# Fourier-layer passes with fewer TensorE instructions, 1 MB transfers and another order of steps

## The chip, the cores and the metric

The kernel runs on one core of a Trainium2 chip. The time is the device time of one execution in microseconds (us), and the median of several runs is quoted. The core has five engines that work side by side, each through its own instructions in order: TensorE (PE, matrix products; its weight loads are listed as PEld), VectorE (DVE), ScalarE (ACT), GpSimd (POOL) and SyncE (SP). SP computes nothing here: it issues most of the DMA transfers, which 16 DMA engines carry between device memory (DRAM) and the on-chip memory SBUF. TensorE writes its results into PSUM, from where DVE and ACT read them. Semaphores order the engines among each other.

## The reference

64 images of 256 x 256 go through a Fourier neural operator with 32 channels and 4 layers. Its output is joined with 77 text rows per image, and one transformer layer (attention and a routed feed-forward part) follows. The part that the change touches is the operator:

```python
v = h @ p_w + p_b                                  # 3 -> 32 channels
for i in range(L):                                 # L = 4
    x_ft = jnp.fft.rfft2(v)                        # only 24 x 12 frequencies are kept
    out1 = jnp.einsum('bixy,ioxy->boxy', x_ft[:, :, :M1, :M2], W1)
    out2 = jnp.einsum('bixy,ioxy->boxy', x_ft[:, :, -M1:, :M2], W2)
    ...
    x1 = jnp.fft.irfft2(out_ft, s=(Sx, Sy))
    x2 = jnp.einsum('bcxy,cd->bdxy', v, w_w[i]) + w_b[i]
    v = x1 + x2
    v = (v - mean) * rsqrt(var + eps) * bn_g[i] + bn_b[i]   # statistics over the whole batch
    if i < L - 1:
        v = relu(v)
out = jnp.einsum('bcxy,cu->bxyu', v, q_w) + q_b
```

Everything is 32-bit floating point. Because the normalisation needs statistics of the whole batch before any value can be normalised, the layers can't be fused for one image: all 64 images pass through one layer before the next begins.

## The kernel before

The program has four kinds of stages. The first (forward_first) takes the input images to their low frequencies. Between layers stands mix (about 160 us in the trace from the last image of one pass to the first of the next), which multiplies the frequencies with the weights and works out the statistics. Three passes (layer, i = 0, 1, 2) turn the mixed frequencies of layer i back into an image, apply normalisation and relu, and take the result forward to the frequencies that the next layer needs. Last comes the transformer, image by image. The change lies in layer. Pass 0 has an order of steps of its own. Passes 1 and 2, the later passes, share one order, and the pass number is i.

**One image in a later pass.** An image is cut into 8 tiles t. A tile is 128 partitions (four row groups of 32 channels) times 8 rows of 256 columns, 1 MB. In DRAM a partition's 8 rows lie together. These are the steps, by the names that the order uses; a digit behind a step is its tile:

- ld (L655): loads the old v of a tile into a vin buffer (4 buffers), as two DMAs of four rows each.
- am (L646): loads the mixed frequencies of an image (ams, two buffers) and scales them on POOL. sp (L663) expands them along x, two matmuls into one ring buffer, spT (L672) transposes that on DVE into y. There are two halves, sp0 for tiles 0 to 3 and sp1 for tiles 4 to 7.
- pre (L681): the new v before relu: 8 matmuls with a 24-row contraction (L687) plus 16 of 32 x 32 that add W v (L698). It allocates the tile's vo buffer (4 buffers).
- evA, evB (L705): relu from PSUM into vo, half a tile each, on ACT (letter a, L710) or DVE (letter d, L712).
- st (L716): stores vo to DRAM, as two DMAs of four rows.
- turn (L721): a 32 x 32 block transpose of vo on DVE (L724) into t32, for the transform along y.
- prod (L729): the next layer's W times v, 16 matmuls of 32 x 32 (L735). Row group n writes PSUM bank ps[n]. sqA and sqB (L741) then sum the squares of the result on ACT (L746), for the variance.
- y0 to y7 (L750): the transform along y over all tiles, 16 matmuls each (L757), all into two ring buffers. half and zt0, zt1 (L764, L770) take the result out through ACT and DVE.
- x (L783): the transform along x, 12 matmuls of 128 x 128 weights times 96 columns (L791) for three groups of frequencies; xo (L800) copies it out on ACT, xs (L807) stores it.

In the profile a 32-bit matmul appears as two MATMUL instructions, each with its own LDWEIGHTS: the 16 of a prod are 32 rows.

**PSUM ring.** The whole of PSUM is four ring buffers of two banks each. take (L605) gives a step the buffers that were closed longest ago: two for pre, prod and y, one for sp and x. close (L617) stands in the eviction step that frees one. So which eviction a matmul step waits for follows from the order alone.

**Order.** ORDER (L128) is written out by hand: one string for pass 0, one for the later passes. The loop at L834 runs the string once per image b; @1 behind a step means that it is done for image b+1, @-1 for image b-1. Each engine executes its own part of this list in exactly this order, and SP issues the DMAs in it, each when what it waits for is done. Steps of different images are thus interleaved: while image b finishes its tiles and its y, image b+1 is begun.

## Time and profile before

| what | value |
|---|---|
| time, median of 3 runs | 11274.06 us (11268.07 to 11280.38) |
| the profiled execution | 11266.44 us, span 11264.7 us, granted TensorE clock 0.984 |
| busy: PE, DVE, ACT, POOL | 10600.1, 8446.4, 6475.0, 1448.0 us |
| PE instructions in the profile | 182550 |
| DMA | 3457.30 MB, mean 307 GB/s |
| pass 0, per image | about 36 us |
| later passes, per image | about 45 us, 128 images |
| transformer, all images | from about 8600 us on |

The profiled execution is one run with the hardware profiler; all durations of instructions come from it. Busy time is the union of the times in which an engine executed something; matmuls are pipelined, and their ends are modelled. The page's 40 slices are 281.6 us each, and a digit is the busy share of a slice in tenths. A line of the groups or of the timeline names the source line, the engine, the operation, the tile written and those read, and the shapes. What stands behind an arrow at the end is what ended the engine's idle time before it. "Share" in a DMA line is the part of the 16 DMA engines' time that the queue's packets took.

### The profile page before, as it was taken

To read this page: it belongs to the slowest core of one execution; us is meant where nothing else is said; L and a number is where in the kernel's file an instruction comes from. 1 tells how busy PE (TensorE), PEld (TensorE's weight loads), DVE (VectorE), ACT (ScalarE), POOL (GpSimd) and SP (SyncE) were. 2 spreads that over 40 slices of the span, in tenths; PEclk is the share of its full clock that TensorE was granted. 3 is DMA by queue.
4 is the path that set the end of the run, shared out by engine and by line. 5 is a ranking of instruction groups with operands and counts; after the bars stand their busy time and mean duration, and the time that the engine had idled before them with its cause. 6 is when DMAs were issued, how large, how long until landed. Compare 5 with 4: busy or idle time off the path is not lost.

```text
span 11264.7 us, 409247 instructions
## 1 busy us (share of the span) xinstructions
PE 10600.1 (94%) x182550; PEld 5728.7 (51%) x182550; DVE 8446.4 (75%) x10381; ACT 6475.0 (57%) x10673; POOL 1448.0 (13%) x2179
## 2 busy tenths in 40 slices
PE   6999999998999999999799999999996999999999
PEld 3555555554444444444444444444443666666666
DVE  6888888887777777777677777777776666666665
ACT  5777777775656555566556566556664333333333
POOL 1111111110000000000000000000000333333333
PEclk8999999998999999999999999999998999999999
DMA  6776676678999999999899999999998555555553
GB/s 214 248 248 246 246 249 246 246 252 322 381 383 384 378 379 375 376 379 379 316 366 386 379 376 381 382 380 378 375 379 301 224 228 228 225 226 227 225 227 137
DMA packets 971776, 3457.30 MB, mean 307 GB/s; under 512 B 149016, under 2 KB 198552, under 8 KB 903064
## 3 DMA queue, kind: packets, MB, share of 16 engines
q1 hardware_dynamic: 904576, 3366.80, 77.7%
q0 software_dynamic: 58288, 60.60, 2.3%
q8 instruction: 1429, 23.41, 0.8%
q10 hardware_dynamic: 7144, 3.72, 0.1%
q14 instruction: 339, 2.78, 0.1%
HBM read 1733.60 MB, written 1696.92 MB: 305 GB/s over the span
## 4 chain that ended last, share of the span: by engine, by line
PE 61%; DMA 21%; DVE 9%; ACT 4%; issue 3%; SPq 2%; POOL 0%; ACTq 0%; DVEq 0%; POOLq 0%
PE ring L757 15%; DMA v<-vo 11%; PE ring L687 9%; PE ring L735 8%; DMA vin<-v 6%; PE ring L698 5%; PE hp L992 4%; PE ring L667 3%; PE pp L1155 3%; PE pp L1166 3%; PE ring L791 2%; PE pp L1120 2%; DVE vo L712 2%; PE pp L1185 2%; DMA xh<-xo 2%
## 5 line engine op out<-in xcount | busy, mean ns | idle before, releaser
L746 ACT ACTIVATE ring<-ring 128x1024 f32<-128x1024 f32 x3072 | 3115.9, 1014 | 1176.6 <-PE ring L735 1114.9
L724 DVE STREAM_TRANSPOSE t<-vo 128x2048 f32<-128x2048 f32 x1536 | 3465.4, 2286 | 21.1 <-DVE vo L712 0.9
L735 PE MATMUL ring<-vo,w 32*32 32x512 f32 x49152 | 2401.5, 599 | 80.3 <-ACT vo L710 64.2
L712 DVE TENSOR_SCALAR vo<-ring 128x1024 f32<-128x1024 f32 x1280 | 1543.8, 1221 | 1191.4 <-PE ring L698 805.3
L710 ACT ACTIVATE vo<-ring 128x1024 f32<-128x1024 f32 x1792 | 1792.2, 1023 | 1039.9 <-PE ring L698 498.1
L757 PE MATMUL ring<-t,cst 32*32 32x512 f32 x49152 | 2063.5, 599 | 46.4 <-issue 40.2
L757 PEld LDWEIGHTS ring<-t,cst 32*32 32x32 f32 x49152 | 909.6, 103 | 917.1 <-issue 615.9
L735 PEld LDWEIGHTS ring<-vo,w 32*32 32x32 f32 x49152 | 801.3, 103 | 1064.7 <-issue 397.6
L687 PE MATMUL ring<-cst,y 24*128 24x256 f32 x16384 | 1232.6, 403 | 76.8 <-DVE vo L712 59.5
L634 POOL TENSOR_TENSOR ams<-ams,bns 48x512 f32<-48x512 f32 x384 | 401.1, 1045 | 6964.8 <-DMA ams<-mix 6692.2
L698 PE MATMUL ring<-vin,ws 32*32 32x512 f32 x32768 | 1278.0, 603 | 17.9 <-issue 14.0
L687 PEld LDWEIGHTS ring<-cst,y 24*128 24x128 f32 x16384 | 789.8, 185 | 992.8 <-DVE vo L712 389.1
L675 DVE STREAM_TRANSPOSE y<-ring 128x1024 f32<-128x1024 f32 x384 | 762.7, 1986 | 320.0 <-PE ring L667 319.0
L687 PE MATMUL ring<-mv,y 29*128 29x256 f32 x8192 | 705.1, 403 | 36.6 <-ACT ring L746 20.2
L687 PEld LDWEIGHTS ring<-mv,y 29*128 29x128 f32 x8192 | 455.9, 185 | 370.2 <-ACT ring L746 209.8
L791 PEld LDWEIGHTS ring<-cst,zt 128*128 128x128 f32 x4608 | 533.6, 193 | 176.7 <-ACT vo L710 113.8
L767 ACT COPY half<-ring 128x1024 f32<-128x1024 f32 x192 | 194.5, 1013 | 723.9 <-PE ring L757 723.9
L1193 POOL DMA_DIRECT2D out_dram<-o x1024 | 511.2, 508 | 664.8 <-DVE o L1188 622.9
L746 ACT ACTIVATION_READ_ACCUMULATOR ring<-ring 128x1 f32 x3072 | 585.4, 191 | 0.0
L791 PE MATMUL ring<-cst,zt 128*128 128x96 f32 x4608 | 565.6, 280 | 6.2 <-DVE zt L775 6.0
L775 DVE STREAM_TRANSPOSE zt<-ring 128x1024 f32<-128x1024 f32 x192 | 377.4, 1965 | 242.8 <-PE ring L757 242.8
L667 PE MATMUL ring<-ams,cst 49*128 49x512 f32 (+1 forms) x1536 | 450.4, 641 | 108.7 <-POOL ams L634 40.1
(374 smaller groups left out, 9759.8 us busy)
## 6 DMA issues: line engine op xcount, KB each, us to landing
v<-vo SPq DMA_DIRECT2D x3072, 512.0 KB, 7.9
vin<-v SPq DMA_DIRECT2D x2048, 512.0 KB, 9.0
ch<-v SPq DMA_DIRECT2D x512, 1024.0 KB, 13.9
mix<-ob SPq DMA_DIRECT2D x48, 1024.0 KB, 5.3
ams<-mix SPq DMA_DIRECT2D x384, 96.0 KB, 8.0
xin<-in_x_dram SPq DMA_DIRECT2D x16, 1024.0 KB, 8.2
mv<-in_x_dram POOLq DMA_DIRECT2D x256, 64.0 KB, 7.2
out_dram<-o POOLq DMA_DIRECT2D x1024, 16.0 KB, 3.1
```

Source lines behind the costliest of these rows:

```text
L667: nc.tensor.matmul(ps[:, n, :], lhsT=EX[hv, 128 * h:128 * h + 128], rhs=ams[b % 2][hv], start=True, stop=True, skip_group_check=True,)
L675: nc.vector.transpose(y_[b, h].rearrange("p q c -> p c q"), ring[key][0][1].rearrange("p n (c k) -> p (n c) k", k=32),)
L687: nc.tensor.matmul(ps[n][:, 256 * r:256 * r + 256], lhsT=y_[b, t // 4][32 * n:32 * n + K, q:q + 4, :].rearrange("p q c -> p (q c)"), rhs=m ...
L698: nc.tensor.matmul(ps[n][32 * j:32 * j + 32], lhsT=ws[32 * n:32 * n + 32], rhs=v[32 * n:32 * n + 32, 2 * j:2 * j + 2, :], start=False, sto ...
L710: nc.scalar.activation(to, ring[key][h][1], AF.Relu)
L712: nc.vector.tensor_scalar(to, ring[key][h][1], 0.0, None, ALU.max)
L724: nc.vector.transpose(t32[b, t // 2][:, :, 8 * (t % 2):8 * (t % 2) + 8, :].rearrange("p y s c -> p s y c"), vo[b, t].rearrange("p s (y l) ...
L735: nc.tensor.matmul(ps[n][32 * j:32 * j + 32], lhsT=w4[i + 1][32 * n:32 * n + 32], rhs=vo[b, t][32 * n:32 * n + 32, 2 * j:2 * j + 2, :], st ...
L746: nc.scalar.activation(ps, ps, AF.Square, accum_out=acc[:, at:at + 1])
L757: nc.tensor.matmul(ps[n][32 * j:32 * j + 32], lhsT=FYT[32 * n:32 * n + 32, k, :], rhs=t32[b, j][32 * n:32 * n + 32, k].rearrange("p s c -> ...
L791: nc.tensor.matmul(ps[:, 0, 96 * g:96 * g + 96], lhsT=zt_[:, h, k0:k0 + 4, :].rearrange("p k c -> p (k c)"), rhs=FX[:, h, 48 * r:48 * r + ...
L1193: nc.gpsimd.dma_start(out[b, 64 * n + 16 * g:64 * n + 16 * g + 16].rearrange("(p t) d -> p t d", t=2), o[32 * g + 8 * n:32 * g + 8 * n + 8 ...
```

## The change

Later passes get these edits:

- **Transfers.** ld is one DMA of 1 MB instead of two of 512 KB, in SP's queue as before; so is st when i is 1 or 2.
- **Wide products.** A prod with the letter w, which the new order uses for tiles 1 and 7, is 8 matmuls of 64 x 64 instead of 16 of 32 x 32. Its weights w64 are built once in a pass: 64 x 64 blocks with W twice on the diagonal and zeros beside it. Both row halves write into the same bank, ps[j], on different partitions.
- **x transform.** Where the order has xt, x takes the table FX as weights (64 columns) and zt as the moving operand (384 columns): 4 matmuls. The result is turned the other way round; xe copies it to SBUF on DVE, and xt turns it back with 3 matmuls against ID2, two stacked identities, which also add the two halves. That makes 7 matmuls instead of 12.
- **Order.** The later passes' string is replaced. Sixteen evictions have the same split as before, 9 on ACT and 7 on DVE. Per image and pass the order now begins with the evictions of pre2, runs pre4, pre5, pre3, pre7, pre0 and pre1 before y0, puts pre6 between y1 and y2, prod1 between y4 and y5, and prod7 behind y7, and ends with pre2 of the image after next. Loads, stores, am and xs move with it.

In pass 0 the order, x and the stores stay as they are.

```diff
 ), (
-    "pre5 sqB7@-1 zt1@-1 sqA7@-1 pre6 evA5.a ld2@1 st4 evB5.d st5 turn4 evA6.a prod5 x@-1 "
-    "evB6.a sqB5 prod6 sqA5 xo@-1 turn5 pre2@1 sqA6 turn6 sqB6 prod4 evA2.a@1 evB2.d@1 "
-    "sqB4 ld0@1 ld7 sqA4 pre0@1 evB0.d@1 ld3@1 prod2@1 st6 evA0.a@1 turn2@1 sqB2@1 sqA2@1 "
-    "pre3@1 ld1@1 evA3.a@1 st2@1 evB3.d@1 pre7 evB7.d prod3@1 ld5@1 evA7.a sqA3@1 turn7 "
-    "pre1@1 st0@1 am@2 sqB3@1 prod0@1 evA1.a@1 evB1.d@1 sqA0@1 st7 sp1@1 st1@1 ld4@1 y0 "
-    "spT1@1 y1 ld6@1 turn0@1 turn3@1 xs@-2 y2 sqB0@1 prod1@1 y3 sqB1@1 sp0@2 y4 sqA1@1 "
-    "spT0@2 y5 y6 st3@1 turn1@1 y7 half.a pre4@1 zt0 prod7 evB4.d@1 evA4.a@1 "
+    "evA2.a@1 evB2.a@1 ld5 ld7 pre4 ld0@1 turn6 prod6 evA4.a x@-1 evB4.d xe.d@-1 turn4 "
+    "sqA6 sqB6 prod4 xt@-1 st2@1 turn2@1 sqA4 pre5 sqB4 xo@-1 am@2 evA5.d evB5.a pre3@1 "
+    "prod2@1 evA3.d@1 turn5 evB3.a@1 st4 sqA2@1 pre7 sqB2@1 evA7.a prod5 evB7.d xs@-1 "
+    "sqB5 pre0@1 ld1@1 st5 sqA5 st3@1 prod3@1 turn7 evB0.a@1 sp1@1 sqA3@1 evA0.d@1 pre1@1 "
+    "sqB3@1 spT1@1 evA1.a@1 prod0@1 ld6@1 sqA0@1 evB1.d@1 ld2@2 sp0@2 spT0@2 y0 ld4@1 y1 "
+    "st1@1 sqB0@1 turn3@1 turn0@1 pre6@1 y2 evB6.d@1 y3 evA6.a@1 y4 prod1.w@1 sqB1@1 st7 "
+    "sqA1@1 y5 st0@1 y6 st6@1 turn1@1 y7 prod7.w half.a zt0 sqA7 sqB7 ld3@2 pre2@2 zt1 "
 )]
...
+    ID2 = const.tile([128, 2 * KX], F32, name="id2")
+    nc.vector.tensor_add(ID2, ID[:, 0:2 * KX], ID[:, 64:64 + 2 * KX])
...
+            w64 = cp.tile([128, 2, C], F32, name="w64")
+            nc.vector.memset(w64, 0.0)
+            for n in range(4):
+                nc.vector.tensor_copy(w64[32 * n:32 * n + 32, n % 2, :], w4[i + 1][32 * n:32 * n + 32])
+            w64 = w64.rearrange("p n o -> p (n o)")
...
+            turned = "xt" in ORDER[min(i, 1)]
...
                 vin[b, t] = ip.tile([128, 8, S], F32, name="vin")
-                for n in range(2):
-                    rows = slice(4 * n, 4 * n + 4)
-                    nc.sync.dma_start(vin[b, t][:, rows], src[b][:, t, rows])
+                nc.sync.dma_start(vin[b, t], src[b][:, t])
...
             def st_(b, t, e):
+                if i:
+                    nc.sync.dma_start(dst[b][:, t], vo[b, t])
+                    return
                 for n in range(2):
...
             def prod(b, t, e):
                 take(("prod", b, t), 2)
                 ps = banks(("prod", b, t))
+                if e == "w":
+                    for j in range(4):
+                        for n in range(2):
+                            m = (n + j) % 2
+                            nc.tensor.matmul(
+                                ps[j][64 * m:64 * m + 64], lhsT=w64[64 * n:64 * n + 64],
+                                rhs=vo[b, t][64 * n:64 * n + 64, 2 * j:2 * j + 2, :], start=True, stop=True,
+                                skip_group_check=True,
+                            )
+                    return
                 for k in range(4):
...
             def x_(b, n, e):
                 zt_ = zts.pop(b)
                 ps = take(("x", b), 1)[0]
+                if turned:
+                    for r in range(2):
+                        for h in range(2):
+                            nc.tensor.matmul(
+                                ps[64 * h:64 * h + 64, 0, 0:384], lhsT=FX[:, h, 48 * r:48 * r + 64],
+                                rhs=zt_[:, h, M * r:M * r + M, :].rearrange("p k c -> p (k c)"),
+                                start=r == 0, stop=r == 1, skip_group_check=True,
+                            )
+                    return
                 for g in range(3):
...
-            xos = {}
+            xos, xes = {}, {}
+
+            def xe(b, n, e):
+                xes[b] = xp.tile([128, 384], F32, name="xe")
+                if e == "a":
+                    nc.scalar.copy(xes[b], ring["x", b][0][1][:, 0, 0:384])
+                else:
+                    nc.vector.tensor_copy(xes[b], ring["x", b][0][1][:, 0, 0:384])
+
+            def xt(b, n, e):
+                xe_ = xes.pop(b)
+                for g in range(3):
+                    nc.tensor.matmul(
+                        ring["x", b][0][1][:, 1, 96 * g:96 * g + 2 * KX],
+                        lhsT=xe_[:, 128 * g:128 * g + 128], rhs=ID2, start=True, stop=True,
+                    )
```

xo then reads the second bank of the ring buffer where the order has xt, and the first as before where it has not.

More of the change, by code (lines that the diff above doesn't have):

```diff
@@ L802, in xo @@
                 nc.scalar.copy(
-                    xos[b], ring["x", b][0][1][:, 0, 0:288].rearrange("p (g k) -> p g k", g=3)[:, :, 0:2 * KX]
+                    xos[b], ring["x", b][0][1][:, int(turned), 0:288].rearrange("p (g k) -> p g k", g=3)[:, :, 0:2 * KX]
                 )
@@ L811, in layer @@
                 am=am, lx=lx, ld=ld, sp=sp, spT=spT, pre=pre, evA=ev(0), evB=ev(1), st=st_, turn=turn,
-                prod=prod, sqA=sq(0), sqB=sq(1), y=y, half=half, zt0=zt(0), zt1=zt(1), x=x_, xo=xo, xs=xs,
+                prod=prod, sqA=sq(0), sqB=sq(1), y=y, half=half, zt0=zt(0), zt1=zt(1), x=x_, xe=xe,
+                xt=xt, xo=xo, xs=xs,
             )
```

## The prediction

> **What bounds the kernel now.** I read the page's slices first. Slices 9 to 19 and 20 to 30 are the two later passes, the only stretch that the new order, the new x and the large transfers touch:
>
> ```profile
> PE   6999999998999999999799999999996999999999
> ...
> DMA  6776676678999999999899999999998555555553
> GB/s 214 248 248 246 246 249 246 246 252 322 381 383 384 378 379 375 376 379 379 316 366 386 379 376 381 382 380 378 375 379 301 224 228 228 225 226 227 225 227 137
> ```
>
> In these passes both TensorE and the DMA engines stand at nine tenths. A window of 2000 us inside one pass, and the DMA view of the same window (packets, MB, share; then transfers, KB, us to landing), say how full. In the first line PE's busy time comes first, then PEld, DVE, ACT, POOL, the granted clock, DMA share and GB/s:
>
> ```profile
> 3400.00:5400.00 2000.00, 1915.79 (x40907) 906.36 (x40912) 1501.38 (x839) 1204.04 (x1897) 92.05 (x88) 1.00 0.98 379
> ```
>
> ```profile
> q1 hardware_dynamic: 215029, 751.33, 97.2%
> ...
> v<-vo SPq DMA_DIRECT2D x706, 512.0 KB, 8.9
> vin<-v SPq DMA_DIRECT2D x704, 512.0 KB, 9.0
> ```
>
> PE is busy 95.8%, DMA 98%. The window has 44.1 images (706 stores, 16 an image), so one image takes 45.35 us. A 512 KB transfer alone would need 1.4 us at 379 GB/s; it lands after 9, so six stand in line: DMA is saturated. Its queue was busy 0.972 x 45.35 = 44.1 us an image, instruction fetches 0.5: a floor of 44.6.
>
> But PE busy counts the tail of every matmul, so I also took the starts of its groups from the timeline:
>
> ```profile
> 4410.14 3.40 PE L757 MATMUL ring<-t,cst 32*32 32x512 f32 x96
> ...
> 4424.00 1.49 PE L735 MATMUL ring<-vo,w 32*32 32x512 f32 x32
> ...
> 4425.49 2.92 PE L791 MATMUL ring<-cst,zt 128*128 128x96 f32 x24
> ...
> 4428.34 1.14 PE L735 MATMUL ring<-vo,w 32*32 32x512 f32 x32
> ...
> 4429.41 1.16 PE L687 MATMUL ring<-cst,y 24*128 24x256 f32 x16
> ...
> 4430.51 1.14 PE L698 MATMUL ring<-vin,ws 32*32 32x512 f32 x32
> ...
> 4431.80 1.02 ACT L710 ACTIVATE vo<-ring 128x1024 f32<-128x1024 f32 x1
> ...
> 4431.86 1.22 DVE L712 TENSOR_SCALAR vo<-ring 128x1024 f32<-128x1024 f32 x1 [1.72 <-PE ring L698]
> ```
>
> Start to start without a wait, a pre is 1.08 (L687) + 0.88 us (L698), a prod 0.88, one y 1.1; a change of array shape adds 0.19 (0.88 becomes 1.07). Evictions start 1.3 us after L698 does; then an ACT pass takes 1.0, a DVE eviction 1.23, turn 2.29, spT and zt 2.0. With four PSUM ring buffers, two for each pre, prod or y, a step waits for the eviction two steps back. From the starts of PE's groups, least (mean) per image: x+prod6 3.92 (3.92), pre2+prod4 3.54 (3.55), pre0+prod2 3.71 (3.90), pre3 2.16 (2.52), pre7+prod3 3.71 (4.12), pre1+prod0 3.45 (3.89), sp1 to y3 6.83 (7.34), sp0 to y7 5.54 (6.02), pre4+prod7 3.71 (4.39), pre5 2.16 (2.24), pre6+prod5 3.45 (3.51). Sum 42.2 (45.4). So the chain through PE, ACT, DVE and the ring could do 42.2; the DMA floor of 44.6 is what holds an image at 45.35. Where the wait appears, the waits of that window show:
>
> ```profile
> ACT vo L710 <- DMA v<-vo: 98.9, 68, 3.3
> ...
> DVE vo L712 <- DMA v<-vo: 93.2, 68, 3.3
> ```
>
> Evictions wait for a store that still reads their vo buffer.
>
> **The change, part by part (us per image of a later pass).**
>
> *1 MB transfers.* 32 issues become 16, the bytes stay; a partition's run goes from 4 KB to 8 KB. In the packet records of the window a 4 KB packet takes 159 ns at best, 168.6 on average. 8 KB packets are in the trace too, the ch loads of the last stage: 309 at best, 319.3 on average. The DMA view there (9500 to 10500 us) agrees:
>
> ```profile
> q1 hardware_dynamic: 32386, 215.24, 53.2%
> ...
> ch<-v SPq DMA_DIRECT2D x200, 1024.0 KB, 13.9
> ```
>
> 215.24 MB in 0.532 of 1000 us is 405 GB/s of busy time, against 751.33 / (0.972 x 2000) = 386 now. Per engine, 255 packets x 168.6 = 43.0 become 127.5 x 319.3 = 40.7, or 41.8 if the excess over the best case (9.6 ns) grows with the bytes (328). With 1.4 for the rest: a floor of 42.1 to 43.3, I take 42.7, a gain of 1.3 to 2.5 in the floor. The nearest row is all reads, hence the far end: no gain. There a rule of the Trainium skill speaks against the change ("DMA: Bandwidth & Descriptors", Specifications): HBM gives one core about 358 GB/s. Were that the limit, packet size would buy nothing and the floor stay at 44.6. The trace moves 379 through both passes, above the figure, and its busy time falls per packet; I go by the rows. A store now waits for both halves of a tile; they are evicted within 0.3 us of each other on two engines, and no store's landing is due sooner than four tiles later.
>
> *x turned.* Removed: 24 instructions x 112 ns = 2.69. Added: 8 of 128x64 by 384 columns. The first stage's L239 has that shape with 512 columns: two column halves run side by side, 429 ns a round. So 4 rounds x 322 = 1.29; then xt, 6 x 112 = 0.67 (128 weight columns as in L791); two more shape changes, 0.4. PE gains 0.3. DVE's xe (128x384, about 0.5 between the 128x144 copy's 0.28 and the eviction's 1.23) holds turn4 behind it, 1.5 us idle before x has landed; turn4 is needed only by y, 20 us on. prod4 stands between x and xt and hides xe.
>
> *Two wide products.* 32 instructions become 16, each of 64x64 with half its weights zero. No row shows 64x64. By L735 the array holds sixteen 32x32 at once (853 ns for 32), so four 64x64 at 429 a round make 16/4 x 429 = 1.72: that end is +0.86 each, plus two shape changes for prod1 and one for prod7. The other end: the two row halves write the same bank (ps[j]), where the old code gives each row group its own (ps[n]). The skill's "TensorEngine Tiling (Array Packing)", PSUM Pressure, says that different row tiles cannot access one bank at the same time; then two run at once, 3.43. Its page "PSUM — Partial Sum Buffer" (bank collisions) quotes that each bank of each partition is a memory of its own, and the halves here never share a partition. No row decides; I take 1.72, as column halves sharing a bank at L239 cost nothing, and keep 3.43 for the range.
>
> *The order.* Priced by the same walk, t from pre2's start, each step at the later of PE free and ring released (0.07 after the eviction ends). pre2 0; pre4 2.15; prod6 4.37 (waits for evA2 and evB2, both ACT behind sqA7, sqB7); x 5.6 (evA4); prod4 7.1; xt 8.2; pre5 9.55 (sqA4); pre3 11.7; prod2 13.66; pre7 15.36 (evA3); prod5 17.3; pre0 19.0 (evB7); prod3 20.96; sp1 22.45; pre1 23.5; prod0 25.72 (spT1); sp0 26.97; y0, y1 28.17; pre6 30.4; y2 to y4 32.4; prod1 wide 36.05 (evB6 behind spT0, turn3, turn0 on DVE: 0.4); y5 to y7 38.0, done 41.1; prod7 wide; pre2 again 2.47 later, when zt0 is done. That is 43.6, against 42.2 for the old order: +1.4, nearly all from the wide products. Of prod7's, 0.37 lies under zt0.
>
> SP's queue, same clock: ld7 2.0 (buffer of pre2), ld0 4.2, st2 4.4, am, st4 5.8, xs 10.8, ld1 13.7, st5, st3 and ld6 15.5, ld2 17.3, ld4 21.0, st1, st7 and st0 27.3, st6, ld3, ld5 36. xs now waits for xo with ld1 behind it, but ld1's buffer is free only at 13.7. st7 sits behind st1 for 8 us; its buffer is asked for at 46. At 2.6 us a transfer, each load lands at least 5 us before its pre, each store 1.5 or more before the eviction that reuses its buffer: tightest st5, 20.4 against evA1 at 25.9, and st2 with evA7, 11 against 17.7. So this order does not wait for DMA. am moves ahead, which drops sp0's wait for ams (30 us in the window, 0.7).
>
> *Setup.* w64 is five small DVE instructions a pass, ID2 one in all: 3 us at most, in front of the first pre.
>
> **Sum.** New image: the chain's 43.6, above the DMA floor of 42.7, plus 0.5 because the two lie within a microsecond of each other (the old pair, 2.4 apart, ran 0.8 over the larger): 44.15. That is 1.1 below the 45.25 of the 124 undisturbed periods, 136 us. The profiled execution took 11266.4 us (span 11264.7, 1.7 around it); it becomes 11130, or 11138 by the median of 11274, which lies 7.6 above.
>
> **Rivals.** (a) The wide products' halves exclude each other: at 3.43 each, prod1 costs 1.7 more and prod7 1.4: 47.2 an image, +2.0 x 124 = 248, 11520, slower. It decides from 2.45 us a product on, where (s - 1.72) + (s - 2.09) eats the 1.1. For it: the shared bank and the cited rule; against: separate partitions. (b) DMA stays the bound: 8 KB packets in a mix of reads and writes are no faster per byte, 45.3, 11270, no change. For it: the 8 KB rows are all reads; against: 9 ns less overhead per 4 KB at best case. (c) PE gains more than streaming says: runs of y take 1.1 a step where prod takes 0.88, with pauses of 0.2 after each 32 matmuls; if those are instruction supply, runs of two or three y, broken by long products, drop them: 43, -2.2 x 124, 11000.
>
> **How the numbers follow.** My case 0.54 (own range 11030 to 11220: 43.3 to 44.9 an image), (a) 0.25, (b) 0.11, (c) 0.10. Less than 0.2% (22 us) either way is not told from no change. Faster: 0.52 of my case and (c), 0.62; same: 0.08, most of (b); slower: (a) and what errs in my case or (b), 0.30. The range 11000 to 11420 leaves out the worst of (a) and the best of (c).
>
> **What would show it.** Right: DMA share near 0.95 and about 390 GB/s in the passes, waits of evictions for v<-vo almost gone, wide product groups 1.7 us from start to start plus 0.2, xt 0.7. Wrong: wide products over 2.4 us; DMA share still 0.98 at 380 GB/s; pre5 waiting for sqA4, or prod1 for evB6, much over the 0.5 given them.

## The result, and the profile after

The changed kernel takes 11214.48 us (median of 4 runs, 11213.23 to 11222.15) against 11273.67 for the kernel before, run beside it: 59 us less, ratio 0.9948 (95% interval 0.9933 to 0.9963). It is faster, by less than half of the 136 us forecast. Run again beside the kernel before, twice, it gave 11206.35 against 11274.82, ratio 0.9938 (0.9923 to 0.9953), and 11214.23 against 11271.06, ratio 0.9945 (0.9928 to 0.9961).

The page's slices of the changed kernel (span 11212.1 us, granted clock 0.984; a slice is 280.3 us). The later passes are again slices 9 to 19 and 20 to 30:

```profile
PE   6999999997999999999799999999997999999999
...
DMA  6767766678999999999899999999997555555553
GB/s 211 248 244 250 248 245 248 247 248 321 377 385 385 379 383 386 389 380 385 316 358 389 380 385 378 390 386 381 386 386 293 227 226 226 226 226 226 226 227 136
```

TensorE and the DMA engines still both stand at nine tenths. The same 2000 us window as before (PE, PEld, DVE, ACT, POOL busy, granted clock, DMA share, GB/s), and then its DMA view:

```profile
3400.00:5400.00 2000.00, 1963.37 (x39629) 844.66 (x39616) 1534.82 (x894) 1222.13 (x1920) 92.04 (x88) 1.00 0.97 384
```

```profile
q1 hardware_dynamic: 115000, 762.21, 95.7%
q8 instruction: 310, 5.08, 0.9%
...
vin<-v SPq DMA_DIRECT2D x357, 1024.0 KB, 11.0
v<-vo SPq DMA_DIRECT2D x357, 1024.0 KB, 9.9
```

357 stores are 44.6 images, where the old window held 44.1. From image to image the steady part of the two later passes takes 44.84 and 44.69 us instead of 45.32 and 45.18: 0.49 less, times 124 periods, 61 us. So the gain lies where the change was made; the two profiled executions as a whole differ by 52 us (11266.4 and 11214.0). The DMA floor, by the forecast's own recipe, is 0.957 x 44.8 = 42.9, plus 0.4 of instruction fetches: 43.3.

Groups of PE and some evictions in the timeline of one image (start, us, then the group):

```profile
4404.71 1.95 PE L745 MATMUL ring<-vo,w 64*64 64x512 f32 x16
...
4406.59 3.40 PE L776 MATMUL ring<-t,cst 32*32 32x512 f32 x96
...
4409.93 1.95 PE L745 MATMUL ring<-vo,w 64*64 64x512 f32 x16
...
4411.80 1.32 PE L693 MATMUL ring<-cst,y 24*128 24x256 f32 x16
...
4417.59 1.51 PE L808 MATMUL ring<-zt,cst 128*64 128x384 f32 x8
...
4419.03 1.14 PE L754 MATMUL ring<-vo,w 32*32 32x512 f32 x32
...
4420.10 0.87 PE L838 MATMUL ring<-id,xe 128*128 128x48 f32 x6
...
4420.90 1.73 PE L693 MATMUL ring<-cst,y 24*128 24x256 f32 x16
...
4430.29 1.02 ACT L716 ACTIVATE vo<-ring 128x1024 f32<-128x1024 f32 x1 [1.03 <-DMA v<-vo]
4430.30 1.22 DVE L718 TENSOR_SCALAR vo<-ring 128x1024 f32<-128x1024 f32 x1 [0.85 <-DMA v<-vo]
```

A wide product (L745) lasts 4406.59 - 4404.71 = 1.88 us from start to start, the second one 1.87. x (L808) takes 1.44, xt (L838) 0.80. And the last two rows show what the forecast's walk did not have: both halves of a tile are evicted a microsecond late because a store still reads their vo buffer. The waits of the window sum these up (total us, times, longest):

```profile
ACT vo L716 <- DMA v<-vo: 25.0, 29, 2.3
...
DVE vo L718 <- DMA v<-vo: 21.8, 29, 2.1
```

Before they were 98.9 and 93.2. They fell to a quarter, and did not go.

All but 1 us of these waits lies at one place: the evictions of pre7, which wait for st4. The built program gives pre7 the vo buffer of pre4, three tiles earlier, and in these cases st4 lands 11.7 us after it is issued (median). In the kernel before, 161 of the 192 us lie at pre3, which has the buffer of pre6, again three tiles earlier, and waits for st6. The second half of pre3 (L698, at 4437.91) and then that of pre7 (4440.30) have started before pre3's evictions can run:

```profile
4437.91 1.39 PE L698 MATMUL ring<-vin,ws 32*32 32x512 f32 x32
...
4440.30 1.16 PE L698 MATMUL ring<-vin,ws 32*32 32x512 f32 x32
4441.01 1.94 ACT L710 ACTIVATE vo<-ring 128x1024 f32<-128x1024 f32 x2 [2.08 <-DMA v<-vo]
4441.03 2.36 DVE L712 TENSOR_SCALAR vo<-ring 128x1024 f32<-128x1024 f32 x2 [2.03 <-DMA v<-vo]
```

The trace has another kind of wait, without a releaser ("issue"): in a run of 32 x 32 matmuls PE now and then stands still. I counted in the records, in 3400:5400 and 6000:8000 together, the gaps of over 0.7 us from the start of one 32 x 32 matmul to the next of the same line. Before they made 72.4 us, 0.82 an image; after, 33.7 us, 0.38 an image. The instructions themselves come by DMA, in packets of 16 KB on queue q8 (5.08 MB for 79,245 PE and PEld instructions, 64 bytes each, so 256 to a packet). In every run these gaps end 2.2 to 2.5 us after the start of the latest such packet (10th to 90th percentile; 2.6 in one). So I take them for late instruction fetches; the runs without stores below bear this out.

### The profile page after: what moved, and what is told of

It is laid out like the page before. It is cut to its first block, busy times and chain, and to the rows that moved or that the text cites. A ratio compares the mean times of both kernels' runs of the same rounds, so it can differ in the third digit from the quotient of the medians.

```text
span 11212.1 us, 395184 instructions
## 1 busy us (share of the span) xinstructions
PE 10666.4 (95%) x177174; PEld 5509.9 (49%) x177174; DVE 8487.2 (76%) x10525; ACT 6483.7 (58%) x10673; POOL 1448.1 (13%) x2179
## 5 line engine op out<-in xcount | busy, mean ns | idle before, releaser
L765 ACT ACTIVATE ring<-ring 128x1024 f32<-128x1024 f32 x3072 | 3112.4, 1013 | 1093.9 <-PE ring L745 612.9
L776 PE MATMUL ring<-t,cst 32*32 32x512 f32 x49152 | 1996.3, 599 | 34.5 <-issue 28.5
L754 PE MATMUL ring<-vo,w 32*32 32x512 f32 x40960 | 1898.8, 601 | 21.0 <-ACT vo L716 19.3
L693 PE MATMUL ring<-cst,y 24*128 24x256 f32 x16384 | 1307.6, 404 | 89.3 <-ACT vo L716 45.5
L776 PEld LDWEIGHTS ring<-t,cst 32*32 32x32 f32 x49152 | 853.0, 103 | 979.5 <-issue 615.2
L693 PEld LDWEIGHTS ring<-cst,y 24*128 24x128 f32 x16384 | 834.7, 185 | 922.5 <-ACT ring L765 246.5
L704 PE MATMUL ring<-vin,ws 32*32 32x512 f32 x32768 | 1196.2, 604 | 0.5 <-issue 0.5
L754 PEld LDWEIGHTS ring<-vo,w 32*32 32x32 f32 x40960 | 648.2, 103 | 845.5 <-issue 441.1
L765 ACT ACTIVATION_READ_ACCUMULATOR ring<-ring 128x1 f32 x3072 | 583.9, 190 | 0.0
L745 PE MATMUL ring<-vo,w 64*64 64x512 f32 x4096 | 506.8, 603 | 1.4 <-issue 1.4
L1036 PE MATMUL hp<-ch,win 128*32 128x512 f32 x4096 | 471.9, 601 | 5.1 <-DMA ch<-v 5.1
L704 PEld LDWEIGHTS ring<-vin,ws 32*32 32x32 f32 x32768 | 249.1, 103 | 351.9 <-issue 350.9
```

What stands on the lines that cost most here:

```text
L693: nc.tensor.matmul(ps[n][:, 256 * r:256 * r + 256], lhsT=y_[b, t // 4][32 * n:32 * n + K, q:q + 4, :].rearrange("p q c -> p (q c)"), rhs=m ...
L704: nc.tensor.matmul(ps[n][32 * j:32 * j + 32], lhsT=ws[32 * n:32 * n + 32], rhs=v[32 * n:32 * n + 32, 2 * j:2 * j + 2, :], start=False, sto ...
L745: nc.tensor.matmul(ps[j][64 * m:64 * m + 64], lhsT=w64[64 * n:64 * n + 64], rhs=vo[b, t][64 * n:64 * n + 64, 2 * j:2 * j + 2, :], start=Tr ...
L754: nc.tensor.matmul(ps[n][32 * j:32 * j + 32], lhsT=w4[i + 1][32 * n:32 * n + 32], rhs=vo[b, t][32 * n:32 * n + 32, 2 * j:2 * j + 2, :], st ...
L765: nc.scalar.activation(ps, ps, AF.Square, accum_out=acc[:, at:at + 1])
L776: nc.tensor.matmul(ps[n][32 * j:32 * j + 32], lhsT=FYT[32 * n:32 * n + 32, k, :], rhs=t32[b, j][32 * n:32 * n + 32, k].rearrange("p s c -> ...
```

## The experiments

The letters in the expectations stand for theories as they stood when each was written; S is told in its own. L and F both hold that the load on the DMA engines is what an image waits for. F is the later and narrower form: the load makes stores land late and instruction fetches come late, on top of a chain through PE, ACT, DVE and the PSUM ring which the change made longer. R and N are about why wide products pay: R says that they break up a run of small matmuls, so that their place counts; N that they are fewer instructions, wherever they stand.

**1 MB transfers alone, in the old order (e_big), and everything but them (e_split).** e_big, on the kernel before:

```diff
                 vin[b, t] = ip.tile([128, 8, S], F32, name="vin")
-                for n in range(2):
-                    rows = slice(4 * n, 4 * n + 4)
-                    nc.sync.dma_start(vin[b, t][:, rows], src[b][:, t, rows])
+                nc.sync.dma_start(vin[b, t], src[b][:, t])
...
             def st_(b, t, e):
+                if i:
+                    nc.sync.dma_start(dst[b][:, t], vo[b, t])
+                    return
                 for n in range(2):
```

> The kernel before with one edit of the change alone: loads and stores of the later passes as one 1 MB transfer. Theory L (the line of transfers holds both kernels; 8 KB packets cost 327 ns among reads and writes, so the floor is about 43.3 us an image): the old order's chain needs only 42.2, so this kernel gains at least as much as the whole change, 44.3 to 44.8 us an image and 11150 to 11220 us. Rival C (the changed kernel is held by its chain through PE, and the new order was needed to use the faster transfers): the old order still waits for its stores and gains less than a third of the change, over 11250.

Measured: 11284.99 us against 11268.97 before, ratio 1.0014 (1.0007 to 1.002). No gain, even slightly slower. Its window and some of its waits:

```profile
3400.00:5400.00 2000.00, 1916.00 (x40912) 908.60 (x40912) 1501.19 (x838) 1204.68 (x1895) 92.04 (x88) 1.00 0.95 378
```

```profile
ACT vo L708 <- DMA v<-vo: 98.7, 62, 3.0
...
DVE vo L710 <- DMA v<-vo: 62.7, 41, 2.9
...
PEld ring L696 <- DMA vin<-v: 36.5, 42, 1.8
...
PE ring L696 <- DMA vin<-v: 19.6, 33, 1.4
```

```profile
v<-vo SPq DMA_DIRECT2D x352, 1024.0 KB, 12.1
vin<-v SPq DMA_DIRECT2D x352, 1024.0 KB, 11.7
```

The DMA share drops from 0.98 to 0.95, so the floor did fall, and the time did not follow. A full load now lands after 11.7 us where its halves took 9.0, a store after 12.1. Evictions wait for stores 161 us instead of 192, but pre (L696 here) now waits 56 us for its load, where before it waited 10.5.

e_split is the mirror, the changed kernel with 512 KB transfers:

```diff
-                nc.sync.dma_start(vin[b, t], src[b][:, t])
+                for n in range(2):
+                    rows = slice(4 * n, 4 * n + 4)
+                    nc.sync.dma_start(vin[b, t][:, rows], src[b][:, t, rows])
...
             def st_(b, t, e):
-                if i:
-                    nc.sync.dma_start(dst[b][:, t], vo[b, t])
-                    return
                 for n in range(2):
```

> The changed kernel with its transfers split into 512 KB again. L: the floor is 44.6 again, an image takes 45.3 or more, 11270 to 11340 us, no better than before. C: the chain of 43 to 43.6 plus its own waits holds, and the time stays within 20 us of the changed kernel's 11214.

Measured: 11278.13, ratio 1.0007 (1.0001 to 1.0014), 64 us above the changed kernel. Evictions wait 50.9 + 48.3 us for stores instead of 25.0 + 21.8, and pre7 with prod5 takes 4.39 us instead of 3.80: that one stretch is 0.59 x 124 = 73 us. So large transfers are worth 64 us in the new order and nothing in the old one. The likely reason is that they land later and need an order that leaves them the time: in e_big the loads come late for pre, in the changed kernel no step waits for a load.

**Plain products for tiles 1 and 7 (e_nowide).**

```diff
-    "st1@1 sqB0@1 turn3@1 turn0@1 pre6@1 y2 evB6.d@1 y3 evA6.a@1 y4 prod1.w@1 sqB1@1 st7 "
-    "sqA1@1 y5 st0@1 y6 st6@1 turn1@1 y7 prod7.w half.a zt0 sqA7 sqB7 ld3@2 pre2@2 zt1 "
+    "st1@1 sqB0@1 turn3@1 turn0@1 pre6@1 y2 evB6.d@1 y3 evA6.a@1 y4 prod1@1 sqB1@1 st7 "
+    "sqA1@1 y5 st0@1 y6 st6@1 turn1@1 y7 prod7 half.a zt0 sqA7 sqB7 ld3@2 pre2@2 zt1 "
```

> The changed kernel with plain 32x32 products for tiles 1 and 7. The chain gets 1.1 to 1.3 us an image shorter. C: the time falls by about that, 124 x 1.2 = 150 us, to 11065. L: the line of transfers still holds, and only 0 to 0.4 us an image come of it, 11165 to 11215.

Measured: 11340.24, ratio 1.0064 (1.0049 to 1.0079): 126 us slower than with wide products. Every theory had them as a price, and taking the price away cost time. A stretch of its timeline, the end of the run from y2 to prod7, and PE's waits in the window, show why:

```profile
4410.97 1.67 PE L776 MATMUL ring<-t,cst 32*32 32x512 f32 x32
...
4414.38 1.89 PE L776 MATMUL ring<-t,cst 32*32 32x512 f32 x47 [1.74 <-issue]
```

```profile
PEld ring L754 <- issue: 194.2, 496, 3.9
...
PE ring L776 <- issue: 41.3, 41, 2.8
```

PE stands for 1.74 us in the middle of y with nothing to wait for but its own instructions; the last packet of them had started at 4412.01, 2.37 us before it went on. In the two windows together such gaps make 216.9 us, 2.5 an image against 0.38. With plain products the run from y2 to prod7 has nothing but small matmuls in it. A group of 32 rows is 64 instructions with its weight loads; a y takes 1.1 us for it and a prod 0.88, so a packet of 256 lasts 3.5 to 4.4 us there.

A long pause costs a second time, through the clock. After one of 2.30 us in the same run the granted clock is at half for 10.2 us, and a pre takes 3.98 us (4554.63 to 4558.61) instead of 1.96:

```profile
4552.49 0.61 PE L776 MATMUL ring<-t,cst 32*32 32x512 f32 x1 [2.30 <-issue]
...
4554.63 2.09 PE L693 MATMUL ring<-cst,y 24*128 24x256 f32 x16 [0.16 <-ACT half L786]
4556.65 2.02 PE L704 MATMUL ring<-vin,ws 32*32 32x512 f32 x32
4558.61 2.09 PE L693 MATMUL ring<-cst,y 24*128 24x256 f32 x16
```

```profile
4554.50:4564.10 9.60, 9.47 (x128) 3.80 (x128) 5.45 (x3) 5.10 (x8) 0.00 (x0) 0.50 0.41 140
```

In 120 steady images of the two later passes e_nowide has 26 such stretches. Of its 97 pauses of 1.7 us or more, from one matmul's start to the next, 24 were followed by one within 5 us, and of its 78 of 1.0 to 1.7 none. The clock time lost (half of each stretch) is 0.57 us an image, which is the most that this can cost: up to 71 us in a profiled execution of 11355. For the other kernels it is 0.33 in e_split (up to 41 us, in one of 11296), 0.21 in w7only and 0.11 in w1only below, at most 0.10 in the rest, 0.03 before and 0.04 after, and nothing in the kernels without stores. So the clock does not bear on the gain of the whole change, but part of what a wide product or a large transfer saves may be this.

**The old x in the new order (e_oldx).**

```diff
-            turned = "xt" in ORDER[min(i, 1)]
+            turned = False
...
             def xe(b, n, e):
+                if not turned:
+                    return
                 xes[b] = xp.tile([128, 384], F32, name="xe")
...
             def xt(b, n, e):
+                if not turned:
+                    return
                 xe_ = xes.pop(b)
```

> The changed kernel with the old x of 12 matmuls in the place of x, and nothing in the places of xe and xt. The chain gets longer by 0.3 us an image on PE and shorter by xe's 0.56 us on DVE. C: +0.3 x 124 = 37 us. L: within 15 us of the changed kernel.

Measured: 11386.61, ratio 1.0103 (1.0088 to 1.0118), 172 us above the changed kernel, or 1.4 us an image. Its timeline:

```profile
4403.18 2.92 PE L819 MATMUL ring<-cst,zt 128*128 128x96 f32 x24
...
4406.02 1.14 PE L754 MATMUL ring<-vo,w 32*32 32x512 f32 x32
...
4407.10 0.70 PE L693 MATMUL ring<-cst,y 24*128 24x256 f32 x4
...
4408.49 1.13 PE L693 MATMUL ring<-cst,y 24*128 24x256 f32 x12 [0.69 <-ACT ring L765]
```

x takes 2.84 us from start to start where x and xt together take 2.24. That is 0.60. The rest is in the last row: pre5 follows prod4 at once, and its second half waits 0.69 us for the squares of prod4 (sqA4, L765), which have to free the ring buffer. From pre5's start to pre3's it is 3.52 us instead of 2.73. In the changed kernel xt stands between prod4 and pre5 and lasts about as long as that wait. So 0.60 + 0.79 = 1.39 an image, 172 us over 124. All of it lies in the chain, which neither expectation had (37 us, or within 15), and the late fetches in 3400:5400 were no more than after (16.8 us, after 18.0).

**Without the stores (n_before, n_after, n_nowide).** To see the chain with less load, three kernels leave out every store of v in passes 1 and 2 and read pass 0's output in both. Half of the traffic is gone, and with it the waits of evictions for a store.

```diff
             def st_(b, t, e):
                 if i:
-                    nc.sync.dma_start(dst[b][:, t], vo[b, t])
                     return
...
-                layer(i, st, vd[(i + 1) % 2], vd[i % 2], acc)
+                layer(i, st, vd[0], vd[0], acc)
```

(In n_before the two lines "if i: return" are added to st_; n_nowide has the order of e_nowide as well.)

> The kernel before without the stores of passes 1 and 2; both passes read what pass 0 stored, so half the traffic is left out, and the result of these passes with it. Theory F (what holds both kernels beyond their chain are waits that loaded DMA engines cause: stores that land late, and instruction fetches that come late in long runs of small matmuls): an image falls to its chain, 42.2 to 42.6 us, the kernel to about 10900. Rival I (the stalls in the runs of y and prod come from PE's own rate of taking instructions and have nothing to do with the load): only the 0.9 us of waits for stores goes, 44.4 an image, 11150.

> The changed kernel without the stores of passes 1 and 2, in the same way. F: the chain, 42.9 to 43.3 us an image, 10990 to 11030, slower than the kernel before is without them. I: 44.2 an image.

> The changed kernel with plain products for tiles 1 and 7 and without those stores. F: the late fetches go, the stretch from pre6 to the end of prod7 falls from 13.65 us to 11.5 to 12, and an image takes 41.9 to 42.3 us, less than with the wide products: they are a loss once fetches are in time. I: that stretch stays at 13.5, and an image takes 45.

Measured, one run each: 10923.08, 11026.65 and 10935.56 us. A window of 1800 us of each, in this order:

```profile
3100.00:4900.00 1800.00, 1754.40 (x39112) 868.60 (x39086) 1439.92 (x801) 1153.21 (x1811) 87.69 (x84) 1.00 0.61 206
```

```profile
3100.00:4900.00 1800.00, 1785.75 (x36772) 782.23 (x36767) 1425.17 (x831) 1138.52 (x1784) 87.82 (x84) 1.00 0.56 203
```

```profile
3100.00:4900.00 1800.00, 1773.90 (x38753) 821.84 (x38751) 1449.59 (x846) 1158.21 (x1819) 87.84 (x84) 1.00 0.58 206
```

With the DMA engines at 0.6 a load lands after 5.1 us in n_after:

```profile
vin<-v SPq DMA_DIRECT2D x333, 1024.0 KB, 5.1
```

No eviction and no matmul waits for a DMA there, and late fetches are almost gone (5.3, 0.9 and 5.2 us in the window). Over the steady part of the two passes an image takes 42.65 us in n_before, 43.38 in n_after, 42.67 in n_nowide. So:

| us per image | before | after | difference |
|---|---|---|---|
| without stores | 42.65 | 43.38 | +0.73 |
| with stores | 45.25 | 44.76 | -0.49 |
| what the load adds | 2.60 | 1.38 | -1.22 |

The starts of PE's groups tell where the load adds it, in the changed kernel (mean us; n_after in 3100:4900, the profile after in 3400:5400):

| stretch | without stores | with stores |
|---|---|---|
| x, prod4, xt, pre5, pre3, prod2 | 9.70 | 9.74 |
| pre7, prod5 | 3.45 | 3.80 |
| pre0, prod3, sp1, pre1, prod0, sp0, y0, y1 | 11.87 | 11.93 |
| pre6, y2 to y4 | 5.48 | 6.09 |
| prod1 wide, y5 to y7 | 5.22 | 5.51 |
| prod7 wide, pre2, pre4, prod6 | 7.67 | 7.67 |
| sum | 43.40 | 44.75 |

0.35 at the one wait for a store, 0.90 in the two stretches with the runs of small matmuls. None of the 0.90 is a wait for an eviction ahead of a wide product: from the start of y4's last matmul to that of prod1, and from y7's to prod7, it is 0.52 us in both kernels. It lies within the y and within prod1.

The kernel before, in 3400:5400 with and without stores (44 and 43 images), shows what became less. There the load adds 1.19 in pre3, pre7 with prod3 and pre1 with prod0, which hold or follow the waits for stores, 1.36 from sp1 to prod7, which is y and what stands between and behind it, and 0.17 elsewhere. So of the difference some 0.84 lies at the waits for stores and 0.46 in the runs around y, where the counted late fetches fell by 0.44.

The change makes the chain longer, and nearly all of that is the wide products: 43.38 against 42.67. Without stores they cost 91 us of the whole time; with them they save 126. (n_after and n_before differ by 104 us as a whole, of which 0.73 x 124 = 91 are these periods; the other 13 are not placed.)

**One wide product at a time (w1only, w7only).** w1only leaves the w off prod7 and w7only off prod1:

```diff
-    "sqA1@1 y5 st0@1 y6 st6@1 turn1@1 y7 prod7.w half.a zt0 sqA7 sqB7 ld3@2 pre2@2 zt1 "
+    "sqA1@1 y5 st0@1 y6 st6@1 turn1@1 y7 prod7 half.a zt0 sqA7 sqB7 ld3@2 pre2@2 zt1 "
```

```diff
-    "st1@1 sqB0@1 turn3@1 turn0@1 pre6@1 y2 evB6.d@1 y3 evA6.a@1 y4 prod1.w@1 sqB1@1 st7 "
+    "st1@1 sqB0@1 turn3@1 turn0@1 pre6@1 y2 evB6.d@1 y3 evA6.a@1 y4 prod1@1 sqB1@1 st7 "
```

> The changed kernel with only tile 1's product wide; tile 7's is plain. The wide product of tile 1 then still cuts the run of 32x32 steps from y2 to prod7 into 3 and 4 groups. Theory R (what a wide product buys is that it breaks a run which instruction fetches can't keep up with): most of the gain stays, 0.1 to 0.4 us an image lost, 11225 to 11265. Rival N (each product that has half the instructions buys half of the 126 us that both bought): 11277.

> The changed kernel with only tile 7's product wide. The run from y2 to y7 stays one of 7 groups, and the wide product comes behind it. R: little of the gain is left, 11310 to 11345. N: 11277, as with tile 1 alone.

The changed kernel ran once more beside them, as a base on the same chip (r_after, no edit):

> The changed kernel once more, unedited, beside the next three: 11214 within 20 us; it gives the size of its own spread for the comparisons.

Measured: r_after 11206.35; w1only 11245.93, ratio 0.9975 (0.9964 to 0.9986), 40 us over r_after; w7only 11285.25, ratio 1.0012 (1.0003 to 1.002), 79 us over it. Losing the wide product inside the y run costs twice what losing the one behind it costs, and the two losses, 119, add up to what losing both cost (126). Late fetches in the two windows are 60.8 us in w1only and 175.9 in w7only. R has the direction: the place counts, and the one that splits the run counts more. Its size for w7only was too large (11310 at least; N's 11277 is nearer), but N's equal halves are out. Up to 26 of the 79 us and 14 of the 40 are the lowered clock told of above.

**Two attempts to improve the order (v_turn0, v_st2).** v_turn0 puts a transpose behind the eviction evB6, for which the forecast had prod1 wait 0.4 us:

```diff
-    "st1@1 sqB0@1 turn3@1 turn0@1 pre6@1 y2 evB6.d@1 y3 evA6.a@1 y4 prod1.w@1 sqB1@1 st7 "
+    "st1@1 sqB0@1 turn3@1 pre6@1 y2 evB6.d@1 turn0@1 y3 evA6.a@1 y4 prod1.w@1 sqB1@1 st7 "
```

> The changed kernel with turn0 of the next image moved on DVE from ahead of evB6 to behind it; nothing asks for turn0 before the next image's y. The wide product of tile 1 waits for evB6, which by the chain ends 0.3 to 0.4 us too late. If that wait is real: 0.2 to 0.5 us an image less, 11150 to 11190. If the stretch is held by instruction fetches: within 12 us of the changed kernel.

Measured: 11256.47, ratio 0.9984 (0.9977 to 0.999), about 42 us slower than the changed kernel. The stretch with evB6, pre6 to y4, did not get shorter (6.14 us on average, 6.09 after), because there was no such wait to remove. From y4's last matmul to prod1 it is 0.52 us with evB6 done 1.7 us or more ahead, as here, or 0.2 us ahead, as in n_after, and it is 0.52 from y7 to prod7 as well, where no eviction is awaited. What is longer is pre7 with prod5 (3.94 us, 3.80 after; evictions wait 67 us for stores in the window instead of 47) and prod1 to y7 (5.68, 5.51 after). Why this edit should lengthen them was not settled.

v_st2 issues the load ld0 behind the store st2 on SP, so that this store goes first:

```diff
-    "evA2.a@1 evB2.a@1 ld5 ld7 pre4 ld0@1 turn6 prod6 evA4.a x@-1 evB4.d xe.d@-1 turn4 "
-    "sqA6 sqB6 prod4 xt@-1 st2@1 turn2@1 sqA4 pre5 sqB4 xo@-1 am@2 evA5.d evB5.a pre3@1 "
+    "evA2.a@1 evB2.a@1 ld5 ld7 pre4 turn6 prod6 evA4.a x@-1 evB4.d xe.d@-1 turn4 "
+    "sqA6 sqB6 prod4 xt@-1 st2@1 ld0@1 turn2@1 sqA4 pre5 sqB4 xo@-1 am@2 evA5.d evB5.a pre3@1 "
```

> The changed kernel with the load of tile 0 issued behind the store of tile 2 instead of ahead of it. evA7 and evB7 wait for that store (the stretch pre7 and prod5 takes 3.80 us loaded and 3.45 without stores), so it lands about 2.6 us earlier: if that wait decides, 0.2 to 0.35 us an image less, 11170 to 11195. If the line of transfers only moves the wait elsewhere: within 15 us of the changed kernel.

Measured: 11311.93, ratio 1.0035 (1.0022 to 1.0048), 105 us slower than r_after. I had taken st2 for the store that pre7 waits for, as in the forecast. It is st4, and with ld0 ahead of it SP issues st4 2.27 us after x's start instead of 0.84. The waits at pre7 rise from 46 us to 71 in the window and pre7 with prod5 takes 4.23 us instead of 3.80. Over 124 images that stretch is 53 of the 105 us; pre0 with prod3 (4.05 instead of 3.78) and pre6 to y4 (6.34 instead of 6.09) have the rest.

**The store that is left (v_am, r2_after).** If that is so, st4 has to be issued earlier. v_am puts am behind it in SP's queue; r2_after is the changed kernel on the same chip.

```diff
-    "sqA6 sqB6 prod4 xt@-1 st2@1 turn2@1 sqA4 pre5 sqB4 xo@-1 am@2 evA5.d evB5.a pre3@1 "
-    "prod2@1 evA3.d@1 turn5 evB3.a@1 st4 sqA2@1 pre7 sqB2@1 evA7.a prod5 evB7.d xs@-1 "
+    "sqA6 sqB6 prod4 xt@-1 st2@1 turn2@1 sqA4 pre5 sqB4 xo@-1 evA5.d evB5.a pre3@1 "
+    "prod2@1 evA3.d@1 turn5 evB3.a@1 st4 am@2 sqA2@1 pre7 sqB2@1 evA7.a prod5 evB7.d xs@-1 "
```

> The edit moves am behind st4 in SP's queue, nothing else; pre7 still takes the vo buffer that st4 reads. Theory S (the store waits that are left lie in one place: the evictions of pre7 wait for st4, which lands 11.7 us after its issue wherever that is; 45.6 us of such waits in the window of the changed kernel): st4 is issued 0.5 us earlier, at 0.3 us after x instead of 0.84, the waits of pre7's evictions fall from 46 us to 25 or less in the window, pre7 with prod5 from 3.80 to about 3.55, and the time falls by 20 to 45 us: 11160 to 11195. Its rival (the DMA engines' load sets when a store lands, not when it is issued): the store lands later after its issue, waits and time stay as they are, 11195 to 11225. In v_st2, which issued st4 1.4 us later, S asks for what was measured, pre7 with prod5 at 4.23.

> The changed kernel without an edit, as the base for v_am on the same chip: 11200 to 11220, pre7 with prod5 3.80.

Measured: v_am 11225.35, ratio 0.9955 (0.994 to 0.997); r2_after 11214.23, ratio 0.9945 (0.9928 to 0.9961). The two do not differ beyond their intervals. The waits of v_am, and of r2_after:

```profile
ACT vo L716 <- DMA v<-vo: 5.1, 9, 0.9
DVE vo L718 <- DMA v<-vo: 4.9, 9, 1.3
```

```profile
ACT vo L716 <- DMA v<-vo: 20.9, 28, 1.7
DVE vo L718 <- DMA v<-vo: 18.4, 28, 1.5
```

Half of S holds. st4 is issued 0.27 us after x, the waits fall to a quarter, and pre7 with prod5 takes 3.56 us instead of 3.74, as S said. But the time does not follow: pre0 with prod3 goes from 3.77 to 3.89, and the image stays at 44.8. The stretches around y are longer by 0.05 each, no more than they differ between two profiles of the unedited kernel. Its rival's mechanism is out (the store did land in time), while its time, up to 11225, fits. So a store that is put off costs time (v_st2), and most of the last wait, taken away, brings none that these runs can tell; where it is given back is only in part seen.

No kernel that was run and still does the whole work is faster than the changed one.

## Why the prediction was right or wrong

The sign was right, the size was not, and the mechanism of the gain was only partly the one forecast. The step that failed is how the load of the DMA engines enters the sum: as a floor, with 0.5 us on top of the larger of two totals. In the changed kernel the load adds 1.38 us to the chain, most of it at one store's landing (0.35) and in the runs of small matmuls around y (0.90).

- **"The DMA floor of 44.6 is what holds an image at 45.35": this failed.** e_big lowered the DMA share to 0.95 at once and gained nothing; with half the traffic an image falls to 42.65, near the 42.2 that the chain's least stretches gave. What lay between was what loaded DMA engines do to the chain: stores that land after some 11 us where their buffer is wanted sooner, and instruction packets that come late in runs of small matmuls. How much that is depends on the order and on the length of those runs, and not only on which of two totals is larger.
- **"Plus 0.5 because the two lie within a microsecond": this is the term that was mis-sized.** What the load adds was 2.60 us before and is 1.38 after. The chain was forecast at 43.6 and measured at 43.38. An image is at 44.76 where the forecast had 44.15: 0.61 x 124 = 76 us, which is what is missing of the 136. The chain is 0.2 better than forecast, and the load term 0.9 worse.
- **"So this order does not wait for DMA": failed in two of its steps.** "No store's landing is due sooner than four tiles later" took the vo buffers to go round in order, so that evA7 would wait for st2. The program gives pre7 the buffer of pre4, three tiles back. And SP was walked at 2.6 us a transfer, each landed before the next: st2, at 4.4, was to be in at 11, which puts st4 at 13.6, before evA7 at 17.7. In the trace several are under way at once. By the same clock (pre2 starts at 4411.80) st4 is issued at 6.6 and lands 11.8 later, at 18.4.
- **1 MB transfers, floor 42.7 of 42.1 to 43.3: the far end.** A packet of 8 KB took 327 ns on average in the window, 328 was the far end, and the floor is 43.3. The nearest row had 319. (That it was all reads need not be the reason: in n_after, whose passes read v and write none, such a packet took 360.) The forecast had looked for a DMA share near 0.95 at 390 GB/s; it is 0.97 at 384. That is still above the 358 GB/s of the rule from "DMA: Bandwidth & Descriptors", Specifications, that was weighed there, which did not decide anything. That these transfers are worth 64 us in this order shows as later landings (0.59 us at pre7 with prod5 in e_split, with the lowered clock behind it); whether the floor of 44.6, which e_split has again, stands behind them no run separates.
- **Wide product 1.72 + 0.19: right.** 1.88 us measured. Two row halves that write one bank on different partitions do not exclude each other, which ends rival (a) and the rule of the Trainium skill's "TensorEngine Tiling (Array Packing)", PSUM Pressure, for this case. The price in the chain is 0.71 (43.38 against 42.67), where the walk had most of 1.4. Missed was that under load they bring more than they cost.
- **x turned, "PE gains 0.3": too small.** PE gains 0.60 (I gave shape changes to the new x only, while the old one, 2.69 by its instructions, took 2.84), and xt fills 0.79 us in which pre5 would otherwise wait for sqA4. The walk did have pre5 waiting for sqA4 at 9.55, about 0.5 us, and pre5 does take 2.73 where its least was 2.16; but I did not ask what the old x would have cost at the same place.
- **prod1 waiting for evB6, 0.4: there is no such wait.** As told under v_turn0, prod1 follows y4 at the same distance wherever evB6 ends. This is part of why the chain is shorter than 43.6.
- **Rival (c)** named the pauses in runs of y as instruction supply, and the runs confirm that such waits exist. But it took them for the fixed cost of a y, 0.2 after every 32 matmuls, to be dropped by a better mix. Those pauses stay without stores: y5 to y7 takes 3.34 us in n_after, 1.11 a step. The late fetches are other and longer gaps. They are all but gone without stores, and in the change they went from 0.82 to 0.38 us an image, 0.44, not 1.1 or more. **Rival (b)** had transfers that bring nothing by themselves: true of e_big, but its reason, packets that cost as much per byte, is not (168 ns for 4 KB, 327 for 8).

Taking any one of the three parts out of the changed kernel costs 64, 126 or 172 us, and the whole change brings only 59. So the new order with none of them would probably be slower than the old kernel; that was not run.

What stays open: the runs without stores take away the traffic and the waits for stores at once, so they tell what both cost together, and by place, but not what traffic alone costs. Of the 0.90 that it still adds around y, gaps of over 0.7 us are 0.4; the others are smaller gaps, which I could not tie to packets. And v_am shows that such waits do not simply add up.

## What to carry to other kernels

When an engine and the DMA engines both stand at nine tenths, the larger of two totals need not be the time. Run the kernel once with part of its traffic taken out, and compare the two stretch by stretch: the difference is what the load adds, and it can sit in a few places, here one reused buffer and the runs of small matmuls. Look up in the built program which buffer a step really gets. Look at the granted clock in windows of a few us too: a mean of 0.98 hid stretches at 0.50 here. Price an edit under the load it will run in, since here one and the same edit cost 91 us without stores and saved 126 with them.

## What the runs showed of the hardware

- **Instruction fetches starve under DMA load.** PE's instructions come in 16 KB packets of 256. In a run of 32 x 32 matmuls a packet is used up in 3.5 to 4.4 us, where the mean of the window is 6.5 (2000 us for 310 packets), and when the next is late PE stands until 2.2 to 2.5 us after that packet's start. With stores this cost 2.5 us an image in e_nowide, without them 0.12.
- **The granted clock can halve behind a pause of TensorE.** In e_nowide 24 of 97 pauses of 1.7 us or more were followed by 3.4 to 10.2 us at a clock of 0.50, none of 78 between 1.0 and 1.7. What decides between those that are followed by it and those that are not was not looked into.
- **Fewer, larger instructions can win though they stream longer.** A 64 x 64 product half of whose weights are zeros takes a microsecond more than the plain one (1.88 against 0.88), and the kernel is 126 us faster with two of them, most of it by the one in the middle of a run.
- **SP held back 512 KB transfers until earlier ones landed.** In the program a DMA of SP signals one of eight semaphores in turn, and waits until the transfer that last used it has landed, so at most eight are under way. SP's own waits in the window of the kernel before, and then after:

```profile
SPq L719 <- DMA v<-vo: 237.2, 263, 2.4
SPq L719 <- DMA vin<-v: 180.1, 207, 2.4
SPq L661 <- DMA vin<-v: 160.4, 151, 2.7
SPq L661 <- DMA v<-vo: 119.9, 132, 2.2
SPq L626 <- DMA vin<-v: 86.4, 89, 2.4
```

```profile
SPq L667 <- PE ring L704: 722.2, 223, 11.5
SPq L724 <- DVE vo L718: 680.6, 178, 7.8
```

  Before, SP waits 784 of 2000 us for other transfers to land before it issues the next one; after, it waits for the engines that fill or free a buffer. e_big has almost none of the first kind left either (38 us) and is no faster, so these waits cost nothing that can be seen by themselves.
